# A graph kernel's square-root table loaded at the start, and the last norm of a layer three steps later among the next hop's operands

## The chip, the cores and the metric

The kernel runs on one core of one Trainium2 chip. The core has engines that work side by side and wait for each other by semaphores: TensorE (in the profile PE for matmuls and PEld for loads of its stationary operand), VectorE (DVE), ScalarE (ACT), GpSimd (POOL), and SyncE (SP), which here only issues DMAs. The metric is the device time in microseconds (us) of one launch.

## The reference

Two layers over a graph of 2048 nodes, a batch of 8 and 64 features. The adjacency matrix `adj` is sparse and symmetric in its pattern, with equal nonzero values within a row. Each layer adds a graph convolution to its input and takes a layer norm over the 64 features.

```python
# layer 0: hops A x and 2 A (A x) - x, mixed with weights that differ for every node
w = einsum('nd,dkio->nkio', embedding, weight)
x_g = einsum('knm,bmc->bnkc', A_stack, x)
x = layernorm(x + einsum('bnki,nkio->bno', x_g, w) + b)
# layer 1: the same A twice, with weights common to all nodes
x1 = A x ; x2 = 2 A x1 - x        # for both supports
x = layernorm(x + concat(x, x1, x2, x1, x2) @ weight + bias)
```

with `layernorm(x) = (x - mean) / sqrt(var + 1e-5)`.

## The kernel before, in words

The 2048 nodes are 16 tiles of 128 rows; a tile holds 8 x 64 = 512 columns (batch and features). Data is split into a high and a low half, which are multiplied by a matrix of zeros and ones (where `adj` is nonzero); the row's value is multiplied in afterwards. So every hop needs, for each step, a high half (`high`, L211, ScalarE), a low half (`low`, L215, VectorE) and a 0/1 matrix (`places`, L200, VectorE; or a cast of stored sums, L546, ScalarE).

The work goes in five stages. They follow each other on TensorE, with the operands of a stage begun during the one before:

1. First hop (0 to about 123 us): plain products, matmuls of L231. `first_constants` stands ahead of it: two DMAs from ScalarE's queue, the constants, and 12 warm-up matmuls on zeros (L135).
2. Second hop (to about 225 us): Strassen's seven products of half matrices (`seven_products`), matmuls of L558.
3. Layer 0's mix (226 to 587 us), tile by tile: `mix0` multiplies a tile's three operands by the node weights into eight PSUM groups `pm` (L361), and adds each group to the accumulator `acc` with four VectorE instructions (L367). Then comes the tile's `layernorm`, and, during the next tile, the transposition of the normed tile (L274, copied out at L276) and its projection by layer 1's weights (`project`, L380, copied out at L387 and L388). PSUM is four tiles of two banks, handed out in turn, so a `pm` waits for the reading of the one four places back.
4. Third hop (587 to about 711 us), again seven products of eight steps each. The operands of its steps 0 to 3 are made early, during layer 0's last four tiles (`early`).
5. Last hop and the final norms (to the end).

`layernorm` is a generator in four pieces. The first sums the rows (L319, L320) and subtracts the mean on GpSimd (L322). The second squares on ScalarE (L310). The third sums the squares (L327), forms the variance (L291, VectorE) and its root (L293, ScalarE). The last takes the reciprocal and one step of refinement (L296, L299, L300, L302, VectorE) and multiplies on GpSimd (L331). The root is the only function that needs a table of its own on ScalarE; the compiler puts a table load ahead of an activation whose function is not in the loaded set.

Two things set the order on an engine. Instructions passed to `ordered` while the list `in_order` isn't empty are pinned behind the instruction that was traced before them on their engine. The others are laid by a planner at compile time, which takes what it thinks is ready. In layer 0's mix the norm's pieces are pinned, while the L367 of the following tile aren't. In the third hop all of it is pinned.

The third hop's order is written out by `run`. At index i it traces the parts of later steps by how far ahead they belong, then step i's own matmuls, then up to two entries of the list `todo`:

```python
return before + [(4, y_high), (3, y_low), (4, load_sum), (2, operands), (0, use)]
```

So at index i stand the sum for step i + 5 (L496; only for products that need one), the high half of step i + 4, the low half of step i + 3, the 0/1 matrix of step i + 2, and the matmuls of step i. For the first product, steps 0 to 7, the 0/1 matrix is made from a slab of `adj` (L200) that SyncE's queue loads into one of five buffers. The next slab goes out when an earlier one's buffer is free.

The last tile's norm takes part in this: its first piece is traced in layer 0's loop, and its other three through `todo`, two entries for each index. Its transposition is traced in step 5's matmul part (`last_transposed`), its projection in step 7's (`last_projected`).

Of the kernel before, what the change touches and what calls it, by code (L numbers as in the profile page):

```python
# [8 lines left out]
F32 = mybir.dt.float32  # L9
# [3 lines left out]
AF = mybir.ActivationFunctionType  # L13
# [4 lines left out]
P = 128  # L18
B, N, C = 8, 2048, 64
# [3 lines left out]
EPS = 1e-5  # L23
# [14 lines left out]
def pattern(  # L38
# [22 lines left out]
    nc = tc.nc  # L61

    def pool(stack, name, bufs, **kw):
        return stack.enter_context(tc.tile_pool(name=name, bufs=bufs, **kw))

    keep = pool(ctx, "fkeep", 1)
    work = pool(ctx, "fwork", 2)
# [14 lines left out]
    def bank(name):  # L82

        return psum.tile([P, 2, 512], F32, tag="ps", name=name)
# [16 lines left out]
    equal = keep.tile([P, 5 * NT], F32, tag="equal", name="equal")  # L101
    nonzero = keep.tile([P, 2 * NT], F32, tag="nonzero", name="nonzero")
    eps = keep.tile([P, 1], F32, tag="eps", name="eps")
    part = keep.tile([P, B], F32, tag="part", name="part")
    rrow = rowpool.tile([P, N], F32, tag="rrow", name="rrow")
    ident = keep.tile([P, P], F32, tag="ident", name="ident")
# [10 lines left out]
    def load(q, to, src):  # L117
        return tc.keep_in_program_order(q.dma_start(out=to, in_=src))
# [8 lines left out]
    def first_constants():  # L127
        load(nc.scalar, z[0][0], x[0].rearrange("n b c -> n (b c)"))
        load(nc.scalar, rcol, rcols)

        idle = spool.tile([P, 5 * P], BF16, tag="s", name="idle")
        nc.vector.memset(idle, 0.0)
        first = bank("first")
        for _ in range(WARM):
            nc.tensor.matmul(first[:, 0, :], lhsT=idle[:, :P], rhs=idle[:, P:], start=True, stop=True)  # L135
        nc.vector.memset(eps, EPS)
        nc.vector.memset(part, 1.0 / C)
        make_identity(nc, ident)

# [96 lines left out]
    todo = []  # L236
# [31 lines left out]
    def transpose(src, tag, pt=None):  # L268

        pt = bank("pt") if pt is None else pt  # L270
        for j in range(B // 2):
            for h in range(2):
                q = slice(h * C, (h + 1) * C)
                nc.tensor.transpose(pt[:, h, j * C : (j + 1) * C], src[q, 2 * j * C : 2 * (j + 1) * C], ident[q, q])  # L274
        tt = work2.tile([P, B // 2, P], F32, tag=tag, name=tag)
        ordered(nc.scalar.copy(  # L276
            tt.rearrange("p j (h n) -> p h j n", h=2), pt[:, :, : B // 2 * C].rearrange("p h (j n) -> p h j n", n=C)
        ))
        return tt
# [60 lines left out]
    def mix0(t, tt, at):  # L340

        acc = work.tile([P, B, C], F32, tag="acc", name="acc")
        for g in range(2):
            part = acc[:, 4 * g : 4 * g + 4, :]
            nc.gpsimd.tensor_tensor(  # L347
                part.rearrange("p (j i) c -> p j i c", j=2),
                bc(0, t)[:, 4 * g : 4 * g + 4, :].rearrange("p (i j) c -> p j i c", j=2),
                ebias[:, t : t + 1, :].unsqueeze(1).to_broadcast([P, 2, 2, C]), ALU.add,  # L350
            )
            for dg in range(D // DG):
                for work_here in at.get((g, dg), ()):
                    work_here()
                ds = slice(dg * DG, (dg + 1) * DG)
                pm = bank("pm").rearrange("p j (i d c) -> p j i d c", i=2, d=DG)
                for i in range(2):
                    for k in range(3):
                        for j in range(2):
                            q = slice(j * C, (j + 1) * C)  # L360
                            nc.tensor.matmul(  # L361
                                pm[:, j, i], lhsT=tt[k][q, 2 * g + i, :], rhs=w[k][q, ds, :],
                                start=(k == 0), stop=(k == 2),
                            )
                for d in range(DG):
                    dd = dg * DG + d
                    ordered(nc.vector.scalar_tensor_tensor(  # L367
                        part, pm[:, :, :, d, :].rearrange("p j i c -> p (j i) c"), emb_sb[:, t, dd : dd + 1], part, ALU.mult, ALU.add
                    ))
        return layernorm(acc)  # L370

    def project(t, hT, pus=None):


        for g in range(2):
            pm = bank("pu") if pus is None else pus[g]
            for i in range(2):
                for j in range(2):
                    q = slice(j * C, (j + 1) * C)
                    nc.tensor.matmul(  # L380
                        pm[:, j, i * 3 * C : (i + 1) * 3 * C], lhsT=hT[q, 2 * g + i, :], rhs=v[q],
                        start=True, stop=True,
                    )
            got = pm[:, :, : 6 * C].rearrange("p j (i k c) -> p j i k c", i=2, k=3)
            to = [bc(k, t)[:, 4 * g : 4 * g + 4, :].rearrange("p (i j) c -> p j i c", j=2) for k in range(3)]
            for k in range(2):
                ordered(nc.scalar.copy(to[k], got[:, :, :, 2 - k, :]))  # L387
            ordered(nc.vector.tensor_tensor(  # L388
                to[2], got[:, :, :, 0, :], bias1.unsqueeze(1).unsqueeze(1).to_broadcast([P, 2, 2, C]), ALU.add,
            ))  # L390
# [4 lines left out]
    BC = B * C // 2  # L395
    KK = NT // 2
    first_constants()


# [206 lines left out]
    def times_r(t):  # L606
        to = z2[:, t, :].rearrange("p (j n) -> p j n", n=P)
        r = rrow[:, t * P : (t + 1) * P].unsqueeze(1).to_broadcast([P, B // 2, P])
        nc.gpsimd.tensor_tensor(to, to, r, ALU.mult)  # L609
# [22 lines left out]
    def operands(t):  # L632
        xt = work2.tile([P, B // 2, P], F32, tag="t0", name="xt")
        load(nc.sync, xt, xT[t])
        return [xt, transpose(z[1][t], "t1"), z[2][t].rearrange("p (j n) -> p j n", n=P)]
# [51 lines left out]
    def early(i):  # L687

        in_order.append(True)
        got = third_got[i] = {}  # L690
        for lead, part in sorted(third[i], key=lambda part: -part[0]):
            if lead > 0:
                part(got)
        third[i] = [part for part in third[i] if part[0] == 0]
        in_order.pop()

    tt, h = operands(0), None
    for t in range(NT):
        done = {}

        def between():
            if t > 0:
                done["hT"] = transpose(h, "hT")
            if t + 1 < NT:
                done["tt"] = operands(t + 1)
            if t + 2 < NT:
                times_r(t + 2)

        at = {(1, 3): [between]}
        if t == NT - 1:  # L710

            in_order.append(True)
            at = {(1, 0): [between], (1, 1): [lambda: project(t - 1, done["hT"])]}
        if t >= NT - 4:
            at[1, 2] = [lambda: early(t - NT + 4)]
        norm = mix0(t, tt, at)
        if t < NT - 1:
            in_order.append(True)
        h = next(norm)
        if t == NT - 1:  # L720
            todo.extend(lambda: next(norm) for _ in range(3))
            break
        tt = done["tt"]
        if t > 0:
            project(t - 1, done["hT"])
        for _ in range(3):
            next(norm)
        in_order.clear()
# [387 lines left out]
def gnn_kernel(tc, x, xT, adj, diag, rcols, bias, pack, w0, out):  # L1116
    nc = tc.nc
    with tc.tile_pool(name="flag", bufs=1) as fpool:
        flag = fpool.tile([1, 1], I32, tag="flag", name="flag")
        odd = pattern(tc, x, xT, adj, diag, rcols, bias, pack, w0, out, flag)  # L1120
        with tc.If(odd > 0):
            general(tc, x, adj, bias, pack, w0, out)
# [49 lines left out]
```

## Time and profile before

| | |
|---|---|
| median of 3 runs | 828.28 us (827.91 to 828.9) |
| the profiled execution | 828.66 us |
| its span in the profile | 826.8 us |
| TensorE busy | 812.6 us, 98% |
| VectorE busy | 594.7 us, 72% |
| ScalarE busy | 275.3 us, 33% |
| GpSimd busy | 111.9 us, 14% |
| ScalarE table loads | 2, of 1.28 us: at 1.67 and at 252.43 us |

The profile is one execution. In its lines "x12" is a count of instructions, "<-" ahead of a name stands for what was read or waited for, and square brackets give the idle time of the engine before a group and what ended it. Matmul ends are modelled: a group of TensorE's seems to run a little into the next one, and the distance of starts is the better measure (0.227 us for a matmul with 512 columns).

### The profile page before, as it was taken

The page shows a single profiled execution, that of the slowest core. Times are in us where ns is not written, and L with a number is a line of the kernel's source. Part 1 is how long each engine was busy: PE and PEld are TensorE (multiplying, and loading weights), DVE is VectorE, ACT ScalarE, POOL GpSimd, SP SyncE. Part 2 cuts the span into 40 slices and gives each one's busy share as a digit, 9 for nine tenths or more (in the row PEclk, how much of TensorE's full clock was granted, in tenths as well). Part 3 has the DMA queues.
Part 4 walks back from the last instruction along what each step waited for, and adds up shares of the span by engine and source line. Part 5 has one row for each costly group of instructions (what it writes and reads, how often), then busy time and mean ns, then how long its engine had stood idle before and what let it go on. Part 6 is the DMA issues. An engine that isn't in the chain of part 4 may idle for free.

```text
span 826.8 us, 14470 instructions
## 1 busy us (share of the span) xinstructions
PE 812.6 (98%) x5614; PEld 725.2 (88%) x5614; DVE 594.7 (72%) x1303; ACT 275.3 (33%) x496; POOL 111.9 (14%) x121
## 2 busy tenths in 40 slices
PE   9999999999999999999999999999999999999995
PEld 6888888888788999999999999999878888888884
DVE  6878658763467888888888888888867546758762
ACT  5436445877401111111111101111287664203110
POOL 0000000000641111111110111111100000003341
PEclk9999999999999999999999999999999999999998
DMA  9997885544200000000000001130154435565631
GB/s 329 376 386 244 287 315 174 155 143 148 69 3 12 15 13 15 14 14 14 14 14 14 30 13 38 39 103 27 43 150 152 141 128 150 167 181 165 212 120 42
DMA packets 70940, 96.54 MB, mean 117 GB/s; under 512 B 4432, under 2 KB 45648, under 8 KB 70736
## 3 DMA queue, kind: packets, MB, share of 16 engines
q1 hardware_dynamic: 61616, 78.49, 29.5%
q10 hardware_dynamic: 6944, 8.66, 3.0%
q0 software_dynamic: 2304, 8.39, 2.8%
q8 instruction: 46, 0.75, 0.4%
q14 instruction: 30, 0.25, 0.1%
HBM read 78.75 MB, written 16.78 MB: 116 GB/s over the span
## 4 chain that ended last, share of the span: by engine, by line
PE 92%; issue 3%; DVE 3%; POOL 1%; ACT 1%; DVEq 0%; POOLq 0%; ACTq 0%
PE pm L361 36%; PE accT L558 24%; PE acc L231 14%; PE a L231 8%; PE accT L231 5%; PE pu L380 2%; DVE acc L367 2%; POOL z L609 1%; PE pt L274 1%; PE accT L662 1%; PE first L135 1%; POOL xc L322 0%; POOL got L337 0%; ACT sq L310 0%; DVE s L200 0%
## 5 line engine op out<-in xcount | busy, mean ns | idle before, releaser
L367 DVE SCALAR_TENSOR_TENSOR acc<-pm,pack_sb,acc 128x256 f32<-128x256 f32 x512 | 246.3, 483 | 41.6 <-PE pm L361 20.5
L558 PE MATMUL accT<-s,hl 128*128 128x512 f32 x896 | 205.6, 390 | 1.9 <-DVE s L200 1.4
L558 PEld LDWEIGHTS accT<-s,hl 128*128 128x128 f32 x896 | 167.6, 188 | 37.7 <-issue 1.8
L361 PE MATMUL pm<-w,xt 64*128 64x256 f32 x1024 | 160.9, 378 | 1.1 <-DVE acc L367 1.1
L361 PE MATMUL pm<-w,t 64*128 64x256 f32 x1024 | 160.0, 376 | 0.2 <-ACT t L276 0.2
L361 PE MATMUL pm<-w,z 64*128 64x256 f32 x1024 | 159.9, 376 | 0.0
L231 PE MATMUL acc<-hl,s 128*128 128x512 f32 x512 | 117.1, 390 | 0.0
L546 ACT CAST s<-raw 128x1024 fp32r<-128x1024 bf16 x96 | 101.0, 1052 | 40.2 <-ACT hl L211 32.2
L231 PEld LDWEIGHTS acc<-hl,s 128*128 128x128 f32 x512 | 95.8, 188 | 21.1 <-DVE hl L215 0.7
L361 PEld LDWEIGHTS pm<-w,t 64*128 64x128 f32 x1024 | 110.7, 187 | 1.9 <-ACT t L276 0.6
L361 PEld LDWEIGHTS pm<-w,z 64*128 64x128 f32 x1024 | 110.8, 187 | 1.4
L361 PEld LDWEIGHTS pm<-w,xt 64*128 64x128 f32 x1024 | 108.4, 187 | 2.5 <-issue 1.2
L276 ACT COPY hT<-pt 128x512 f32<-128x512 f32 x15 | 8.8, 587 | 197.4 <-PE pt L274 197.4
L231 PE MATMUL a<-hl,s 128*128 128x512 f32 x320 | 73.0, 389 | 0.0
L231 PEld LDWEIGHTS a<-hl,s 128*128 128x128 f32 x320 | 60.0, 188 | 12.5
L211 ACT CAST hl<-z 128x256 fp32r<-128x256 f32 (+1 forms) x96 | 47.1, 510 | 67.6 <-PE acc L231 36.4
L215 DVE TENSOR_TENSOR hl<-z,hl 128x512 fp32r<-128x512 f32 (+1 forms) x96 | 52.5, 552 | 21.2 <-ACT hl L211 18.4
L322 POOL TENSOR_TENSOR xc<-acc,s 128x512 f32<-128x512 f32 x16 | 16.7, 1043 | 279.5 <-DVE s L320 265.4
L200 DVE TENSOR_SCALAR s<-raw 128x1024 fp32r<-128x1024 f32 x47 | 33.2, 706 | 16.5 <-PE acc L231 10.9
L231 PE MATMUL accT<-hl,s 128*128 128x512 f32 x192 | 44.2, 390 | 0.0
L231 PEld LDWEIGHTS accT<-hl,s 128*128 128x128 f32 x192 | 35.9, 188 | 7.4
L347 POOL TENSOR_TENSOR acc<-z,ebias 128x256 f32<-128x256 f32 x32 | 22.7, 731 | 90.5 <-DVE hl L215 87.2
(105 smaller groups left out, 603.3 us busy)
## 6 DMA issues: line engine op xcount, KB each, us to landing
raw<-in_adj SPq DMA_DIRECT2D x67, 512.0 KB, 4.7
raw<-sums_of SPq DMA_DIRECT2D x64, 256.0 KB, 2.8
sums_of<-z POOLq DMA_DIRECT2D x16, 512.0 KB, 6.3
raw<-quarters SPq DMA_DIRECT2D x32, 256.0 KB, 2.6
raw<-in_adj SPq DMA_DIRECT2D x16, 384.0 KB, 3.5
quarters<-seen ACTq DMA_DIRECT2D x16, 256.0 KB, 6.2
xt<-in_xT SPq DMA_DIRECT2D x16, 256.0 KB, 2.6
out<-got ACTq DMA_DIRECT2D x16, 256.0 KB, 3.9
```

Of the source, the lines that this page charges most:

```text
L200: ordered(nc.vector.tensor_scalar(s, raw, 0.0, None, ALU.not_equal))
L211: ordered(nc.scalar.copy(to[0], src))
L215: ordered(nc.vector.tensor_tensor(to[1], src, to[0], ALU.subtract))
L231: nc.tensor.matmul(accs[i], lhsT=s[:, i * P : (i + 1) * P], rhs=hl[h], start=(first and h == 0), stop=(last and h == 1),)
L276: ordered(nc.scalar.copy(tt.rearrange("p j (h n) -> p h j n", h=2), pt[:, :, : B // 2 * C].rearrange("p h (j n) -> p h j n", n=C)))
L322: ordered(nc.gpsimd.tensor_tensor(xc, src, wide(s), ALU.subtract))
L347: nc.gpsimd.tensor_tensor(part.rearrange("p (j i) c -> p j i c", j=2), bc(0, t)[:, 4 * g : 4 * g + 4, :].rearrange("p (i j) c -> p j i c", ...
L361: nc.tensor.matmul(pm[:, j, i], lhsT=tt[k][q, 2 * g + i, :], rhs=w[k][q, ds, :], start=(k == 0), stop=(k == 2),)
L367: ordered(nc.vector.scalar_tensor_tensor(part, pm[:, :, :, d, :].rearrange("p j i c -> p (j i) c"), emb_sb[:, t, dd : dd + 1], part, ALU.m ...
L380: nc.tensor.matmul(pm[:, j, i * 3 * C : (i + 1) * 3 * C], lhsT=hT[q, 2 * g + i, :], rhs=v[q], start=True, stop=True,)
L546: ordered(nc.scalar.copy(s, got["raw"]))
L558: nc.tensor.matmul(acc[i][:, c], lhsT=hl[h][:, i * P : (i + 1) * P], rhs=S[:, c * 512 : (c + 1) * 512], start=(kk == 0 and h == 0), stop=( ...
```

## The change

Two edits. In `first_constants` the constant `eps` is written ahead of the warm-up's zeros, and ScalarE takes the square root of it into an otherwise unused column, pinned behind its two DMA issues: the first function on ScalarE is now the square root. In layer 0's last tile, the three remaining pieces of the norm go into `todo` with five empty entries between the first and the second. With two entries for each index, the squares stay at index 0, the sum of squares with the root moves from index 0 to index 3, and the last piece from index 1 to index 3.

```diff
+    root = work.tile([P, B], F32, tag="ln_s", name="root")[:, :1]
...
         load(nc.scalar, rcol, rcols)
+        nc.vector.memset(eps, EPS)
+
+        tc.keep_in_program_order(nc.scalar.activation(root, eps, AF.Sqrt))

         idle = spool.tile([P, 5 * P], BF16, tag="s", name="idle")
         nc.vector.memset(idle, 0.0)
         first = bank("first")
         for _ in range(WARM):
             nc.tensor.matmul(first[:, 0, :], lhsT=idle[:, :P], rhs=idle[:, P:], start=True, stop=True)
-        nc.vector.memset(eps, EPS)
         nc.vector.memset(part, 1.0 / C)
...
         if t == NT - 1:
-            todo.extend(lambda: next(norm) for _ in range(3))
+
+            todo.extend([lambda: next(norm)] + [nothing] * 5 + [lambda: next(norm)] * 2)
             break
```

## The prediction

> **What bounds the kernel now.** I read the page's busy line first, then TensorE's waits, then the timeline around the two places that the change touches.
>
> ```profile
> PE 812.6 (98%) x5614; PEld 725.2 (88%) x5614; DVE 594.7 (72%) x1303; ACT 275.3 (33%) x496; POOL 111.9 (14%) x121
> ```
>
> TensorE is the bound, so a change is worth what it takes from TensorE's idle time. Its waits (total us, times, longest):
>
> ```profile
> PE accT L558 <- DVE s L200: 1.4, 1, 1.4
> ...
> PE pm L361 <- DVE acc L367: 1.1, 1, 1.1
> PE accT L558 <- DVE z L388: 0.6, 1, 0.6
> ```
>
> Between the warm-up and the tail these three are nearly all there is, about 3 us, and that is the ceiling of any gain here. The second is at 267.22, in tile 1 of layer 0's mix, soon after the table load. The first is at 595.91, where the last norm stands among the third hop's operands. The timeline around the table load (start, duration, engine, line):
>
> ```profile
> 251.78 0.63 ACT L310 ACTIVATE sq<-xc 128x512 f32<-128x512 f32 x1 [6.25 <-POOL xc L322]
> 252.43 1.28 ACT L293 ACT_TABLE_LOAD   x1
> 253.72 0.30 ACT L293 ACTIVATE ln_sd<-ss,eps 128x8 f32<-128x8 f32 x1
> ...
> 252.44 0.69 DVE L327 TENSOR_REDUCE ss<-sq 128x8 f32<-128x512 f32 x1 [1.87 <-ACT sq L310]
> 253.16 0.17 DVE L291 SCALAR_TENSOR_TENSOR ln_v<-ss,eps 128x8 f32<-128x8 f32 x1
> 254.05 0.20 DVE L296 RECIPROCAL ln_r<-ln_sd 128x8 f32<-128x8 f32 x1 [0.72 <-ACT ln_sd L293]
> 254.17 0.45 DVE L367 SCALAR_TENSOR_TENSOR acc<-pm,pack_sb,acc 128x256 f32<-128x256 f32 x1
> 254.54 0.16 DVE L299 SCALAR_TENSOR_TENSOR ln_q<-ln_r 128x8 f32<-128x8 f32 x1
> ```
>
> The load runs beside the reduction L327 and outlasts it; VectorE then stands 0.72 us. From 254.05 to 267.09 VectorE works on tile 1's accumulations with one 0.46 us hole, and the one that ends at 267.09 frees the PSUM bank that TensorE waits for (1.05 us). Tile 0 alone mixes the norm's small steps with L367; the other tiles run L296, L299, L300, L302, and then L367. The same timeline around the last norm:
>
> ```profile
> 591.97 0.69 DVE L327 TENSOR_REDUCE ss<-sq 128x8 f32<-128x512 f32 x1 [1.89 <-ACT sq L310]
> ...
> 593.90 0.42 DVE L215 TENSOR_TENSOR hl<-z,hl 128x256 fp32r<-128x256 f32 x1
> 594.12 1.09 POOL L331 TENSOR_TENSOR xc<-xc,ln_r 128x512 f32<-128x512 f32 x1 [2.85 <-DVE ln_r L302]
> 594.23 1.53 DVE L200 TENSOR_SCALAR s<-raw 128x1024 fp32r<-128x1024 f32 x1
> ...
> 595.91 3.94 PE L558 MATMUL accT<-s,hl 128*128 128x512 f32 x16 [1.36 <-DVE s L200]
> 599.78 0.46 PE L274 MATMUL accT<-ident,xc 64*128 64x64 f32 x8
> 600.17 3.92 PE L558 MATMUL accT<-s,hl 128*128 128x512 f32 x16
> ```
>
> Step 4's 0/1 matrix (L200) is queued behind the whole norm on VectorE, and takes 1.53 us where the others take 0.69, while GpSimd's multiply L331 runs. TensorE, done with steps 0 to 3, waits for it.
>
> **What the Trainium skill says.** "ScalarE: Activation LUTs", What ACT_TABLE_LOAD costs: about 1283 ns a load, and some 1380 ns of draining. The trace has the 1.28; it shows no drain, as the load starts 0.02 us behind the square and the root 0.01 behind the load. Table sets (same page): cheap functions such as copy are in every set. The trace agrees: casts, copies and squares run for 570 us after the root's load without a third one. "SBUF — State Buffer", Who interferes with whom: VectorE and GpSimd share a port pair; a VectorE instruction with two SBUF inputs, or in a two-port mode, is blocked for the whole of a GpSimd instruction that reads SBUF. The trace agrees: the L200 above, and an L215 at 212.98 that took 1.14 us for 0.42 beside a GpSimd L609. Both ended 0.3 to 0.55 us after the GpSimd instruction.
>
> **Part 1, the table.** At the start: the same single load at 1.67, now for the root's set; an added Sqrt of 128x1, priced by the row of 128x8 at 0.30 us; the small constant `eps` (0.06 us) is written ahead of the warm-up's zeros. The Sqrt would end near 3.3 us, and ScalarE stands 2.01 us until the first cast at 4.96, which waits for a DMA. So zero; without that cover 0.3. Both ScalarE DMA issues (0.73 and 1.18) stay ahead of the load. The warm-up starts 0.06 us later, ahead of a first real matmul that waits for the cast: zero, at most 0.06. The two-buffered tile that Sqrt writes is wanted again 248 us later.
>
> At tile 0: the load of 1.28 goes, but 0.72 of it lies beside L327. The root then starts as in tile 14, with L291 (both at 569.06, the reciprocal at 569.39, 0.33 later): root at 253.16, reciprocal at 253.49 in place of 254.05, 0.56 us earlier. If the order on VectorE stays, all that follows is 0.56 earlier, with its inputs there (pm of tile 1's groups are ready over a microsecond before), and TensorE's stall falls from 1.05 to 0.49: **gain 0.56**.
>
> The order is the uncertain thing. Tile 1's L367 aren't pinned to the norm; a planner mixes them. If it lays tile 0 like the other tiles, L367 comes 1.78 to 1.88 us after L327's start (274.91 to 276.69; 297.47 to 299.35), so at 254.22 to 254.32. The fourth is then three times 0.517 later, near 255.82 in place of 255.70: loss 0.12. Tile 0 differs from its fellows in two ways: the load, and that TensorE has no projection (1.30 us) ahead of its next product. Either can explain the mixing; the second stays. I take the order as kept, with both ends in the range: -0.12 to +0.56.
>
> **Part 2, the norm.** The square stays at step 0. The reduction, its variance, and the root go from step 0 to the end of step 3, the rest of the norm and the multiply from step 1 to step 3. None of it issues a DMA. The root passes three casts on ScalarE; GpSimd has nothing else queued. On VectorE seven norm instructions go behind the low half (L215) and L200 of steps 4 and 5, the low half of step 6 and step 8's two sums (L496).
>
> New VectorE order, by the pitches that the trace shows after 595.69 (L200 0.60, L496 0.46 and 0.34, L215 0.33): low half of step 4 at once at 590.03. GpSimd's subtract, which starts at 590.23, may wait some 0.06 for it, so the square runs at 591.36. Step 5's high half is queued behind the square on ScalarE: cast at 591.88, low half 592.31, L200 of step 4 at 592.64, **done 593.33**. TensorE's step 4 can start when steps 0 to 3 are through: 587.01 plus 32 times 0.227 is 594.29, in place of 595.91. Stall gone, 1.62 us won so far.
>
> What is late next: step 8's sums 593.24 and 593.70, low half of step 6 594.04, L200 of step 5 594.37 to 595.06 (needed at 596.11: in time), then the norm: L327 594.97, L291 and root 595.69, L296 596.02, L299 596.26, L300 596.46, L302 596.70. The multiply follows L302 by 0.31: 597.01 to 598.10. TensorE reaches the transposes of it at 594.29 plus 16 times 0.227 plus 0.23, 598.16: just in time. Step 9's sums start at 596.79; the second, due at 597.25, has two SBUF inputs and is held until the multiply ends, so ends near 598.38, 0.71 later than due. Low half of step 7 at 598.30, L200 of step 6 598.63 to 599.32. TensorE's step 6 follows by 0.14: 599.46, where it would otherwise start at 598.55. It stood at 600.17 before. **Gain 0.71**; the hold takes 0.71 and VectorE's pace 0.20 of the 1.62. Step 7's L200 is ready at 601.15, wanted at 601.28. The wait on L388 (0.56) and the projection's evictions move along: ScalarE is free at about 603.2, a microsecond ahead of them. SP's slab of step 7 waits for step 4's L200 (595.76, issued 595.79), so goes out near 593.4, earlier, in a stretch of light traffic. From 612 to 810 TensorE shows no gap: what is won at 606 reaches the end.
>
> Bounds: without a hold on L496, 1.42; if also the subtract, the casts or L200 of step 6 are held once more by 0.3 to 0.4, 0.35.
>
> **Sum.** 0.56 + 0.71 = 1.27. The profiled execution took 828.66 (span 826.8 and 1.86 around it): 827.39. It lies 0.38 above the median of the runs, 828.28: 827.01.
>
> **Rivals.**
> (a) Tile 0's order becomes that of the others: -0.12 + 0.71 = 0.59, 827.7. For it: fourteen tiles look so. Against it: the missing projection explains the mixing without the load.
> (b) The multiply holds nothing on VectorE: 0.56 + 1.42 = 1.98, 826.3. For it: the first sum, already running, may keep the ports, and GpSimd's L331 was only 0.05 longer beside an L215. Against it: the two held instructions above.
> (c) Slower: the planner lays the last hop otherwise. Its L810 (1.29 us each, twenty) aren't pinned; one put behind a tile's eviction, sum and norm (0.75 + 0.68 + five times 0.17 to 0.20 and the waits at 804 to 806, some 3.5 us) could starve TensorE once by up to 3.5 less a slack of about 1. Two of these, near 5 us, less 1.27: 832. It decides from 2.93 us of new stalls (1.27 + 1.66). For it: small shifts reach the planner. Against it: no dependency there is touched.
> (d) The load isn't saved, since the copies bring their own set back: 0.71 alone, 827.6. Against it: one set served all of them after 252.43.
>
> **How the numbers follow.** 0.2% is 1.66 us, about what a measurement of this kernel can tell from no change. Chances: forecast 0.40, (a) 0.25, (b) 0.20, (c) 0.07, (d) 0.03, something unseen that gains more, up to the 3 us ceiling, 0.05. Faster by over 0.2%: (b) and the unseen, and about a quarter of the forecast's share, since 0.39 us more than my sum, less than the spread of the runs (0.99), lifts it over: 0.35. Slower: 0.07. Same: 0.58. Range: from (b) with 0.4 of spread, 825.9, to (a) with 0.6 of it, 828.3.
>
> **What would show it.** One table load in the whole trace, near 1.7. At tile 0 a reciprocal at 0.33 us behind the root, and the pm wait at 0.5 (at 1.2 if (a)). No wait of L558 on L200 ahead of step 4, and a new one of some 0.9 ahead of step 6, with an L496 of over 1 us beside L331; without that, (b). Wrong: the transposes wait for the multiply by over 0.2, a third load, or a new wait after 612.

## The result, and the profile after

The changed kernel takes 827.23 us (median of 22 runs, 826.82 to 827.85) where the kernel before takes 828.39 (22 runs, 827.91 to 828.9): 1.16 us less, a ratio of 0.9987 with a 95% interval of 0.9981 to 0.9992. That is faster, but by less than 0.2%; the interval leaves room for 0.7 to 1.6 us, so the sizes of the parts below are read from the traces. The profiled execution took 826.98 us, its span 825.2 (before: 828.66 and 826.8). From its line 140 on, the changed file numbers most lines three higher: the former L200 is L203, L361 is L364, L558 is L561.

The page's busy line has hardly moved; TensorE's waits have. First the busy line, then the waits (total us, times, longest), of the kernel after:

```profile
PE 812.4 (98%) x5614; PEld 725.2 (88%) x5614; DVE 594.9 (72%) x1303; ACT 274.1 (33%) x496; POOL 112.4 (14%) x121
```

```profile
PE accT L561 <- ACT hT L279: 0.8, 1, 0.8
PE accT L561 <- DVE z L391: 0.6, 1, 0.6
PE pm L364 <- DVE acc L370: 0.5, 1, 0.5
```

The wait on the accumulation near 266 is 0.5 in place of 1.1. The one ahead of step 4 (1.4) is gone; there is one of 0.85 ahead of step 6, which the view puts down to ScalarE's copy of the transposed tile. The timeline of the kernel after, at tile 0 of layer 0's mix (start, duration, engine, line):

```profile
251.66 0.63 ACT L313 ACTIVATE sq<-xc 128x512 f32<-128x512 f32 x1 [6.24 <-POOL xc L325]
253.04 0.30 ACT L296 ACTIVATE ln_sd<-ss,eps 128x8 f32<-128x8 f32 x1 [0.75 <-DVE ss L330]
...
252.32 0.69 DVE L330 TENSOR_REDUCE ss<-sq 128x8 f32<-128x512 f32 x1 [1.87 <-ACT sq L313]
253.04 0.17 DVE L294 SCALAR_TENSOR_TENSOR ln_v<-ss,eps 128x8 f32<-128x8 f32 x1
253.38 0.20 DVE L299 RECIPROCAL ln_r<-ln_sd 128x8 f32<-128x8 f32 x1 [0.17 <-ACT ln_sd L296]
253.50 0.46 DVE L370 SCALAR_TENSOR_TENSOR acc<-pm,pack_sb,acc 128x256 f32<-128x256 f32 x1
253.87 0.16 DVE L302 SCALAR_TENSOR_TENSOR ln_q<-ln_r 128x8 f32<-128x8 f32 x1
253.99 0.48 DVE L370 SCALAR_TENSOR_TENSOR acc<-pm,pack_sb,acc 128x256 f32<-128x256 f32 x1
```

No table load stands between the squares and the root. The reciprocal comes 1.06 us after the sum of squares started, where it came 1.61 after it before; and the norm's small steps still alternate with the accumulations L370. The only load is at the start, and the added root takes 0.20 us there:

```profile
1.67 1.28 ACT L133 ACT_TABLE_LOAD   x1 [1.67 <-PEq L1166]
2.96 0.20 ACT L133 ACTIVATE root<-eps 128x1 f32<-128x1 f32 x1
```

And the timeline around the last norm, VectorE and TensorE, and one line of GpSimd:

```profile
591.64 0.43 DVE L218 TENSOR_TENSOR hl<-z,hl 128x256 fp32r<-128x256 f32 x1 [1.90 <-ACT hl L214]
591.98 0.69 DVE L203 TENSOR_SCALAR s<-raw 128x1024 fp32r<-128x1024 f32 x1
...
594.31 0.68 DVE L330 TENSOR_REDUCE ss<-sq 128x8 f32<-128x512 f32 x1
...
596.60 1.15 DVE L499 TENSOR_TENSOR t<-t,z 128x256 f32<-128x256 f32 x1
597.67 0.41 DVE L218 TENSOR_TENSOR hl<-z,hl 128x256 fp32r<-128x256 f32 x1
598.00 0.68 DVE L203 TENSOR_SCALAR s<-raw 128x1024 fp32r<-128x1024 f32 x1
...
586.33 11.17 PE L561 MATMUL accT<-s,hl 128*128 128x512 f32 x48
597.52 0.46 PE L277 MATMUL accT<-ident,xc 64*128 64x64 f32 x8
598.83 3.93 PE L561 MATMUL accT<-s,hl 128*128 128x512 f32 x16 [0.85 <-ACT hT L279]
...
596.37 1.09 POOL L334 TENSOR_TENSOR xc<-xc,ln_r 128x512 f32<-128x512 f32 x1 [5.72 <-DVE ln_r L305]
```

TensorE now runs steps 0 to 5 as one block of 48 matmuls and waits behind the transposes. Step 4's 0/1 matrix (591.98) takes 0.69 us and is in time. What is stretched now is the second sum of step 9, L499: 1.15 us for 0.42, beside GpSimd's multiply.

Now the starts on TensorE, of the kernel before (two lines) and after (one line; its third hop is above):

```profile
225.55 0.46 PE L274 MATMUL pt<-ident,z 64*128 64x64 f32 x8
587.01 7.55 PE L558 MATMUL accT<-s,hl 128*128 128x512 f32 x32
...
225.43 0.46 PE L277 MATMUL pt<-ident,z 64*128 64x64 f32 x8
```

The third hop begins 0.68 earlier (587.01 to 586.33), of which 0.12 were there when the mix began (225.55 to 225.43) and some 0.55 come from tile 0. Over the profiled executions of this document the mix begins anywhere from 225.43 to 226.15, so starts are compared as distances within one execution. Step 6 begins 1.34 earlier (600.17 to 598.83), so the last norm gave 0.66. (The view's waits, 1.36 gone and 0.85 new, differ by less, because the modelled ends run into them. By starts the old wait is the 1.62 of the prediction, and the new one 0.92: step 6 begins 1.31 after the transposes where it began 0.39 after them.) The last matmuls begin 1.36 earlier (813.16 to 811.80), and so does the issue of the last DMA to within 0.01 (821.73 to 820.36). The remaining 0.24 of the spans' 1.6 lies behind that, where nothing was changed. 0.55 + 0.66 = 1.21 stands beside the 1.16 of the medians.

### The profile page after: what moved, and what is told of

It is laid out like the page before. It is cut to its first block, busy times and chain, and to the rows that moved or that the text cites. A ratio compares the mean times of both kernels' runs of the same rounds, so it can differ in the third digit from the quotient of the medians.

```text
span 825.2 us, 14469 instructions
## 1 busy us (share of the span) xinstructions
PE 812.4 (98%) x5614; PEld 725.2 (88%) x5614; DVE 594.9 (72%) x1303; ACT 274.1 (33%) x496; POOL 112.4 (14%) x121
## 4 chain that ended last, share of the span: by engine, by line
PE 95%; DVE 2%; issue 1%; ACT 1%; POOL 0%; POOLq 0%; DVEq 0%; ACTq 0%
PE pm L364 39%; PE accT L561 23%; PE acc L234 14%; PE a L234 8%; PE accT L234 5%; PE pu L383 2%; DVE acc L370 1%; PE pt L277 1%; PE accT L665 1%; PE first L139 1%; POOL got L340 0%; DVE t L499 0%; DVE s L203 0%; ACT sq L313 0%; POOL xc L325 0%
## 5 line engine op out<-in xcount | busy, mean ns | idle before, releaser
L370 DVE SCALAR_TENSOR_TENSOR acc<-pm,pack_sb,acc 128x256 f32<-128x256 f32 x512 | 246.3, 484 | 41.6 <-PE pm L364 21.0
L561 PE MATMUL accT<-s,hl 128*128 128x512 f32 x896 | 205.3, 390 | 1.4 <-ACT hT L279 0.8
L561 PEld LDWEIGHTS accT<-s,hl 128*128 128x128 f32 x896 | 167.7, 188 | 36.7 <-ACT hT L279 1.0
L364 PE MATMUL pm<-w,xt 64*128 64x256 f32 x1024 | 161.0, 378 | 0.5 <-DVE acc L370 0.5
L364 PE MATMUL pm<-w,t 64*128 64x256 f32 x1024 | 160.1, 376 | 0.2 <-ACT t L279 0.2
L364 PE MATMUL pm<-w,z 64*128 64x256 f32 x1024 | 160.0, 376 | 0.0
L364 PEld LDWEIGHTS pm<-w,t 64*128 64x128 f32 x1024 | 110.7, 187 | 2.1 <-ACT t L279 0.6
L364 PEld LDWEIGHTS pm<-w,z 64*128 64x128 f32 x1024 | 110.8, 187 | 1.5
L364 PEld LDWEIGHTS pm<-w,xt 64*128 64x128 f32 x1024 | 108.3, 187 | 2.0 <-PE pt L277 0.6
L203 DVE TENSOR_SCALAR s<-raw 128x1024 fp32r<-128x1024 f32 x47 | 32.3, 688 | 15.9 <-PE acc L234 11.7
```

Of the source, the lines that this page charges most:

```text
L203: ordered(nc.vector.tensor_scalar(s, raw, 0.0, None, ALU.not_equal))
L364: nc.tensor.matmul(pm[:, j, i], lhsT=tt[k][q, 2 * g + i, :], rhs=w[k][q, ds, :], start=(k == 0), stop=(k == 2),)
L370: ordered(nc.vector.scalar_tensor_tensor(part, pm[:, :, :, d, :].rearrange("p j i c -> p (j i) c"), emb_sb[:, t, dd : dd + 1], part, ALU.m ...
L561: nc.tensor.matmul(acc[i][:, c], lhsT=hl[h][:, i * P : (i + 1) * P], rhs=S[:, c * 512 : (c + 1) * 512], start=(kk == 0 and h == 0), stop=( ...
```

## The experiments

The theory: two independent gains, each set by a wait of TensorE. The rivals: the gain is the table's or the norm's alone; the mixed order at tile 0 doesn't matter; step 6 waits for ScalarE's copy, as the view of waits has it, and not for the 0/1 matrix that GpSimd's multiply delays. The first four kernels ran together, with a median of 828.50 for the kernel before; the other four with 828.46.

### The table alone

```diff
-            todo.extend([lambda: next(norm)] + [nothing] * 5 + [lambda: next(norm)] * 2)
+            todo.extend(lambda: next(norm) for _ in range(3))
```

> Only the table is loaded first; the norm stays at indices 0 and 1. Theory (two independent gains, 0.55 at tile 0 and 0.66 at the last norm): TensorE's wait on L370 near 267 falls from 1.05 to 0.50 us as in the changed kernel, the wait ahead of step 4 stays at 1.36 with an L203 of about 1.5 us, and the time is about 0.55 us under the kernel before, 827.8. Rival (the stretch near 595 absorbs what is won at tile 0, or the whole gain is the norm's): the time is the kernel before's, and the first wait of L561 grows to about 1.9.

Measured: 827.75 us, 0.75 less than before; ratio 0.9992 (0.9984 to 1.0000). TensorE's waits in its profile:

```profile
PE accT L561 <- DVE s L203: 1.4, 1, 1.4
...
PE pm L364 <- DVE acc L370: 0.5, 1, 0.5
```

As the theory has it: the wait near 266 falls to 0.5, the one ahead of step 4 stays at 1.36. The interval touches 1, so the size of 0.55 rests on the trace. There the last matmuls begin 587.03 us after the mix (225.54 to 812.57), where they began 587.61 after it before: 0.58 won, and the stretch near 595 absorbs none of it.

### The norm alone

The change in `todo` without the two lines that take the root of `eps` and the moved constant.

> Only the norm is moved; the root's table is loaded at tile 0. Theory: the wait on L367 stays at 1.05, the wait ahead of step 4 is gone, one of about 0.85 ahead of step 6 is there, and the time is about 0.66 us under the kernel before, 827.7. Rival: without the earlier start the norm is too late for the transposes and TensorE waits for the multiply; then step 6 starts less than 0.3 us earlier than before, against the start of the third hop.

Measured: 827.65 us, 0.85 less than before; ratio 0.9990 (0.9983 to 0.9996). Its waits:

```profile
PE pm L361 <- DVE acc L367: 1.0, 1, 1.0
PE accT L558 <- ACT hT L276: 0.8, 1, 0.8
```

And TensorE in its timeline:

```profile
586.95 11.17 PE L558 MATMUL accT<-s,hl 128*128 128x512 f32 x48
...
599.45 3.91 PE L558 MATMUL accT<-s,hl 128*128 128x512 f32 x16 [0.85 <-ACT hT L276]
```

Step 6 begins 12.50 us after the third hop (586.95 to 599.45), as in the changed kernel (586.33 to 598.83), where it was 13.16 before: 0.66 won. The rival, under 0.3, falls. In the traces the two parts add: about 0.55 and 0.66 alone, and the same two together. The medians can't show it: 0.75 and 0.85 alone, each within 0.2 of the traces, would make 1.60, and 1.16 was measured.

### The order of the other tiles, at tile 0

```diff
-                    ordered(nc.vector.scalar_tensor_tensor(
+                    step = nc.vector.scalar_tensor_tensor(
...
-                    ))
+                    )
+                    if in_order or (t, g, dd) == (1, 0, 0):
+                        tc.keep_in_program_order(step)
```

> The changed kernel with the first accumulation of tile 1 pinned behind the first norm, so that VectorE runs L299, L302, L303, L305 and then the accumulations, as in the other tiles. Theory (the gain at tile 0 rests on the mixed order): the first accumulation starts 1.78 to 1.88 us after the sum of squares instead of 1.18, the fourth about 0.67 us later than in the changed kernel, and TensorE's wait near 267 is about 1.15 to 1.2 us: 0.65 us slower than the changed kernel, about 827.9. Rival (the order doesn't matter, the table load alone did it): wait near 0.5 and the changed kernel's time, 827.2.

Measured: 827.93 us; ratio 0.9994 to the kernel before (0.9986 to 1.0002). Its timeline on VectorE and its wait:

```profile
253.03 0.69 DVE L330 TENSOR_REDUCE ss<-sq 128x8 f32<-128x512 f32 x1 [1.87 <-ACT sq L313]
...
254.09 0.20 DVE L299 RECIPROCAL ln_r<-ln_sd 128x8 f32<-128x8 f32 x1 [0.17 <-ACT ln_sd L296]
...
254.73 0.17 DVE L305 SCALAR_TENSOR_TENSOR ln_r<-ln_q,ln_r 128x8 f32<-128x8 f32 x1
254.82 1.52 DVE L370 SCALAR_TENSOR_TENSOR acc<-pm,pack_sb,acc 128x256 f32<-128x256 f32 x3
```

```profile
PE pm L364 <- DVE acc L370: 1.1, 1, 1.1
```

The accumulations start 1.79 us after the sum of squares, against 1.18 in the changed kernel; TensorE's wait is back at 1.1. Without any table load in the way, the gain at tile 0 is gone. What was won there hangs on an order that the planner chose, and that nothing in the program asks for. (This order with the load still in place was not run.) The traces also show where the 0.6 comes from. In the mixed order the accumulations start 0.49 to 0.52 us apart (253.50, 253.99, 254.51, 255.03) with a small step of the norm between each two. In an unbroken row they are no closer: eight of them take 4.19 us here, 0.53 from start to start. So between accumulations the small steps cost VectorE no time, while in a row they hold it from 254.09 to 254.82.

### Without GpSimd's multiply

```diff
-        ordered(nc.gpsimd.tensor_tensor(xc, xc, wide(next(root)), ALU.mult))
+        r = next(root)
+        if not skip:
+            ordered(nc.gpsimd.tensor_tensor(xc, xc, wide(r), ALU.mult))
```

with `skip` true for the last tile.

> The changed kernel without GpSimd's multiply of the last tile's norm: that tile goes on unscaled, nothing else changes. Theory (the multiply holds VectorE's second sum L499 by the shared ports, 1.15 instead of 0.42 us, and so the 0/1 matrix of step 6): no L499 over 0.45 us, L203 of step 6 done 0.7 us earlier, TensorE's wait ahead of step 6 about 0.1 to 0.2 instead of 0.85, and the time about 0.7 under the changed kernel, 826.5. Rival (step 6 waits for ScalarE's copy of the transposed tile, as the profile's waits put it): the copy is no earlier than 0.1 us, the wait stays near 0.85 and the time at 827.2.

Measured: 826.51 us; ratio 0.9976 (0.9968 to 0.9985); 0.83 less than the changed kernel by the differences to before (1.99 and 1.16). Its timeline, VectorE, ScalarE and TensorE:

```profile
596.84 0.43 DVE L501 TENSOR_TENSOR t<-t,z 128x256 f32<-128x256 f32 x1
597.18 0.42 DVE L218 TENSOR_TENSOR hl<-z,hl 128x256 fp32r<-128x256 f32 x1
597.51 0.69 DVE L203 TENSOR_SCALAR s<-raw 128x1024 fp32r<-128x1024 f32 x1
...
598.23 0.59 ACT L279 COPY hT<-accT 128x512 f32<-128x512 f32 x1 [0.47 <-PE accT L277]
...
598.35 3.91 PE L563 MATMUL accT<-s,hl 128*128 128x512 f32 x16 [0.21 <-DVE s L203]
```

The sum takes 0.43 again, and step 6's wait falls from 0.85 to 0.21. Step 6 begins at 598.35, while ScalarE's copy runs until 598.82: so it doesn't wait for that copy. In the changed kernel the copy ended at 598.73 and the 0/1 matrix at 598.68, and the view named the later of the two. In both kernels step 6 starts 0.15 us after the end of its 0/1 matrix (598.20 to 598.35, and 598.68 to 598.83).

### The squares one step later

```diff
-            todo.extend([lambda: next(norm)] + [nothing] * 5 + [lambda: next(norm)] * 2)
+            todo.extend([nothing] * 2 + [lambda: next(norm)] + [nothing] * 3 + [lambda: next(norm)] * 2)
```

> The changed kernel with the last norm's squares at index 1 instead of index 0, so behind ScalarE's cast of step 5's high half, which is then made long before. Theory (the 1.9 us that VectorE stands ahead of step 5's low half, behind the squares, is the start of the chain that makes step 6 late): the 0/1 matrix of step 4 is done about 1.1 us earlier than in the changed kernel, that of step 6 about 1.2 us earlier, TensorE's wait ahead of step 6 is gone, and the time is 0.85 us under the changed kernel, about 826.4. Rival (the multiply's hold sets step 6 wherever the chain starts, or a new wait comes behind it at step 7 or in front of the projection): a wait of over 0.4 stays before 606 besides the one on L391, and the time is 826.9 or more.

Measured: 826.32 us; ratio to the kernel before 0.9975 (0.9965 to 0.9985). Its timeline:

```profile
589.57 1.60 DVE L218 TENSOR_TENSOR hl<-z,hl 128x256 fp32r<-128x256 f32 x2
591.09 0.68 DVE L203 TENSOR_SCALAR s<-raw 128x1024 fp32r<-128x1024 f32 x1
...
595.70 1.15 DVE L499 TENSOR_TENSOR t<-t,z 128x256 f32<-128x256 f32 x1
...
597.11 0.68 DVE L203 TENSOR_SCALAR s<-raw 128x1024 fp32r<-128x1024 f32 x1
...
586.57 11.17 PE L561 MATMUL accT<-s,hl 128*128 128x512 f32 x48
597.67 0.46 PE L277 MATMUL accT<-ident,xc 64*128 64x64 f32 x8
598.06 3.92 PE L561 MATMUL accT<-s,hl 128*128 128x512 f32 x16
```

Step 6's 0/1 matrix is done 11.22 us after the third hop's start (586.57), 1.13 earlier than in the changed kernel (598.68 less 586.33), and step 6 follows the transposes with no wait. The multiply's hold is still there (L499 at 595.70, 1.15 us), but it no longer reaches TensorE. The move has a price of its own: the two low halves at 589.57 take 1.60 us together, since the second, from 589.90 to 591.17, is now held by GpSimd's subtract (589.79 to 590.89). That hold is shorter than the 1.9 us of standing that it replaces.

### The norm at index 4, and at index 2

```diff
-            todo.extend([lambda: next(norm)] + [nothing] * 5 + [lambda: next(norm)] * 2)
+            todo.extend([lambda: next(norm)] + [nothing] * 7 + [lambda: next(norm)] * 2)
```

> The changed kernel with the norm's last two pieces at index 4 instead of 3. Theory (index 3 ends just in time): the multiply ends some 1.7 us later, near 599.2, TensorE waits for it ahead of the transposes by about 1.7 us, which is 0.85 us more than the wait it replaces, and the time is about 0.85 over the changed kernel, 828.1. Rival (the wait ahead of step 6 merely trades places with one ahead of the transposes, as the 0/1 matrix of step 6 is then early): within 0.3 of the changed kernel.

Measured: 827.60 us; ratio 0.9990 (0.9983 to 0.9996). TensorE in its timeline:

```profile
586.66 11.63 PE L561 MATMUL accT<-s,hl 128*128 128x512 f32 x50
599.58 0.46 PE L277 MATMUL accT<-ident,xc 64*128 64x64 f32 x8 [1.30 <-POOL xc L334]
599.98 3.47 PE L561 MATMUL accT<-s,hl 128*128 128x512 f32 x14
603.37 1.57 PE L383 MATMUL accT<-v,hT 64*128 64x192 f32 x16
```

The transposes do wait for the multiply, by 1.3 us, but the loss is only 0.35 by the start of the projection (603.37 less 586.66, against 602.69 less 586.33), and not 0.85. In the medians it is 0.37. The reason is in the counts: 50 matmuls ahead of the transposes and 14 behind, where the changed kernel has 48 and 16. The planner put two of step 6's matmuls ahead, which need nothing of the norm. It was free to: in the third hop the operands are pinned, as said further up, but the matmuls are not. The direction was right. The size missed by more than half, and lies nearer to the rival's 0.3: the wait ahead of step 6 is gone, and most of what came ahead of the transposes only takes its place.

The edit for index 2 has `[nothing] * 3` in the same place.

> The changed kernel with the norm's last two pieces at index 2. Theory (VectorE's work between step 4's and step 5's 0/1 matrices then holds the norm, the multiply, and the hold on step 8's second sum): step 4 starts without a wait, step 5 waits about 1.6 us for L203, and the time is about 0.65 over the changed kernel, 827.9, nearly the kernel with the table alone. Rival (any place after step 4's matrix gives the same): within 0.2 of the changed kernel.

Measured: 827.81 us; ratio 0.9994 (0.9986 to 1.0002). Its wait:

```profile
597.27 2.08 PE L561 MATMUL accT<-s,hl 128*128 128x512 f32 x8 [1.48 <-DVE s L203]
```

Step 5 waits 1.48 us, and the projection comes 0.74 later after the hop's start than in the changed kernel (603.53 less 586.43). The rival, under 0.2, falls. So with the squares at index 0, index 3 is the best of the three by the traces, with a loss on either side.

### Both remaining waits

The kernel with the squares later, and besides the norm of tile 0 resumed inside tile 1:

```diff
+        if t == 1:
+            def rest(norm=norm):
+                in_order.append(True)
+                for _ in range(3):
+                    next(norm)
+                in_order.clear()
+            at[0, 1] = [rest]
         norm = mix0(t, tt, at)
...
-        for _ in range(3):
-            next(norm)
+        if t > 0:
+            for _ in range(3):
+                next(norm)
```

> The kernel with the squares at index 1, and besides the last three pieces of tile 0's norm traced after the first group of tile 1's accumulations, so that VectorE runs these four in the 1.87 us in which it waits for the squares. Theory (TensorE's remaining wait of 0.5 near 266 is VectorE's time lost in that place): the wait on L370 is gone, the other waits are as in the kernel with the squares later, and the time is about 0.5 under it, 825.9. Rival (the norm of tile 0, now later, makes the transposition of tile 0 wait, or the time is lost again ahead of the third hop): a new wait of some 0.5 between 266 and 590, and no gain.

Measured: 825.92 us; ratio 0.9969 (0.9958 to 0.9981), 2.54 less than before, 0.40 less than with the squares later alone, and the lowest of all. Its timeline on VectorE at tile 0, and all of TensorE's waits but the warm-up's:

```profile
250.59 2.04 DVE L370 SCALAR_TENSOR_TENSOR acc<-pm,pack_sb,acc 128x256 f32<-128x256 f32 x4
252.55 0.69 DVE L330 TENSOR_REDUCE ss<-sq 128x8 f32<-128x512 f32 x1
```

```profile
PE accT L561 <- DVE z L391: 0.6, 1, 0.6
PE pm L364 <- ACT t L279: 0.2, 1, 0.2
```

Four accumulations fill the 1.87 us in which VectorE waited for GpSimd and ScalarE, and the wait near 266 is gone. The third hop begins 360.34 us after the mix (225.66 to 586.00), against 360.90 with the squares later alone (225.67 to 586.57), and no new wait came in between: the rival falls. Of the three waits of the kernel before, only the projection's is left.

## Why the prediction was right

**The bound.** It held: TensorE's busy time moved by 0.2 us, and the time followed its waits. 827.01 was forecast, 827.23 measured; 1.27 us of gain forecast, 1.16 measured, the forecast's own case. The other 0.11 is the base, 828.28 then and 828.39 in the runs beside the changed kernel.

**The start.** The added root took 0.20 us where 0.30 was taken from the wider row, and hid where it was said to, ahead of a first cast at 5.44. The warm-up began at 1.28 in place of 1.25. The first real matmul came at 6.11 in place of 5.63, but it did so in the kernel with the norm alone too (6.05), whose start is unchanged, and the mix began no later (225.43 against 225.55).

**Tile 0.** Root to reciprocal is 0.34 us; 0.55 was won for 0.56, and TensorE's wait is 0.49. The uncertain step was the order, and it stayed mixed. The kernel with the other tiles' order shows what that was worth: 0.6 of wait. It is the rival that ends at 827.7, 0.59 under the kernel before, and it took 827.93, 0.57 under it. Since the order stayed though the load went, the load isn't needed for the mixing; that the missing projection causes it was argued and isn't shown. So the forecast took the right order without shown ground for it, and in that it was partly lucky.

**The last norm.** 0.71 forecast, 0.66 measured. With the 0.68 of the earlier start added, VectorE's times in the trace agree with the forecast's within 0.1 us from end to end: step 4's matrix at 592.66 (592.64 forecast), the multiply at 597.05 (597.01), the held sum's end at 598.43 (598.38), step 6 at 599.51 (599.46). Most of the 0.05 comes with the root, which began 0.78 us after the sum of squares where the row used for it has 0.72. The hold, which I took from two stretched instructions of the trace before, came on the instruction named, with 1.15 us; the kernel without the multiply shows that it cost 0.64 of wait. So the rival without a hold falls. That the multiply causes the hold is shown by leaving it out; that it does so by shared ports is not tested by any run here. The forecast speaks of seven norm instructions on VectorE; there are six, as its own list of starts has it, and the root runs on ScalarE.

**Just in time.** The view shows no wait of the transposes; the multiply ended at 597.46, 0.06 ahead of them. By starts they touch the edge: they begin 11.19 us after the hop (586.33 to 597.52), and 11.10 after it where the multiply is left out or done earlier (586.57 to 597.67 in both). The 0.09 costs nothing here, as step 6 waits for its 0/1 matrix anyway. The kernel at index 4 shows the loss behind this edge, smaller than computed for it.

**What fell.** The load came once, and the last hop shows no wait. The prediction's list of signs was met but for one word: the view of waits names the copy and not the 0/1 matrix for step 6. Had I read only that view, I would have called the mechanism wrong.

## What to carry to other kernels

Where one engine is 98% busy, list its waits, and price a change by which of them it ends and what is late next; removing a 1.28 us load gave 0.55, and 1.62 us of earlier start gave 0.66. When an item is moved along a queue, replay the queue from the trace's own distances of starts, with what one engine holds up on another; here that foretold each start within 0.1 us. And ask what stands idle in front of the chain: filling VectorE's 1.9 us behind the squares gained 1.01 in the traces (step 6 comes 11.49 after the hop's start instead of 12.50), more than the 0.66 of the move itself.

## What the runs showed that was not expected

- The view of waits can name an innocent one when two things end 0.05 us apart (598.68 and 598.73); taking one of them away settled it.
- The planner moved two matmuls (0.227 us each) across the transposes when the norm went to index 4; about 0.5 of the 0.85 us of computed loss did not come. An order that isn't pinned can soften a change as well as spoil it.
- Which instruction is held depends on what VectorE starts while GpSimd's is running: the same multiply held a 0/1 matrix by 0.84 us before, and a sum by 0.73 after. A sum that was running already when the multiply started (596.15) took its usual 0.42, and GpSimd then took 1.09 for 1.04. The prediction states the rule without this order. A held instruction ended at GpSimd's end plus its own usual time less about 0.14 (595.76 after 595.21; 597.75 after 597.46; 591.17 after 590.89). Only where this reaches TensorE's next operand does it cost.
